# First taps of the tail's depthwise chains made on ScalarE, and a new pace for the work beside the samplings

## The chip, the cores and the metric

The kernel runs on one core of one Trainium2 chip. The metric is device time in microseconds (us), the median of several executions. Engines are named as the profile names them: PE (TensorE's matmuls; PEld its weight loads), DVE (VectorE), ACT (ScalarE), POOL (GpSimd), SP (the queue that issues plain DMAs).

## The reference

Four layers run one after the other on a batch of 4 images of 256 channels and 64 x 64 pixels, all in float32. Each is applied to a group-normalised input and added to its residual:

```python
x = x + L0(_gn(x))   # 1x1 conv; deformable 3x3 sampling in 4 groups (36 points a pixel, bilinear); feed-forward with squeeze-excite
x = x + L1(_gn(x))   # linear attention: qkv 1x1 conv, a 5x5 depthwise conv of qkv, two sums over pixels, projection
x = x + L2(_gn(x))   # 3x3 conv with binarised weights
x = x + L3(_gn(x))   # softmax attention of 4096 pixels to 1024 pooled ones
```

The change bears on three places: the 5x5 depthwise convolution of layer 1 (`agg`), whose 25 taps are summed per channel; the work that runs beside the sampling of layer 0; and the loads of the feed-forward's weights.

## The kernel before, in words

After a head, `run` (from L1348 on) works image by image. `sample(n)` gathers the deformable sampling of image n in 288 rounds: `gathered` issues four indirect DMAs from GpSimd into one of 7 `g` buffers (L607), and PE reduces them with 16 small matmuls (L614). Results are copied by ACT (L619), turned by PE (L624), spread into `dT` by ACT (L634), and, after every 18 rounds, a block is projected (`project`, L647), added to the image (`add`, L653 and L654) and scaled, with a sum for the squeeze-excite mean kept in `ssum` (`finish`, L658).

Beside the rounds of one image, other works of earlier images advance. `beside(steps, number, *works)` takes works as (generator, total cost, lo, hi): after step i of `number`, the share i/number is compared with what each work has spent of its total between lo and hi, and a work that lags is advanced. Costs are numbers written by hand in the generators' `yield`s. Within `ordered()` the instructions of PE, DVE, ACT and POOL run in exactly the order in which the generators write them; the order of SP's DMAs is left to the framework.

- Beside `sample(0)`: the convolution of images 1 to 3 and their offsets.
- Beside `sample(1)`: the binarised weights, then `feedforward(0)` (share 0 to 0.22) and `layer1(0)` (0.22 to 1).
- Beside `sample(2)` and `sample(3)`: `feedforward` and `layer1` of the image before, and `second` of the one before that (layers 2 and 3, from 0.22 to 1).

The feed-forward begins with four loads of weights (L704 to L710: f1 and f2 of 1 MB each, sd, su), takes the mean of `ssum` (L712), goes through two small matmuls (L716, L723), scales f1 on ACT (L727) and then runs its big matmuls (L752, L762). Its buffers lie on the right side of SBUF, where those of `layer1` lay before it.

The tail begins after `sample(3)`. `self.alone` is set, and 900 empty steps carry `feedforward(3)` (share 0 to 0.27), `layer1(3)` (0.27 to 1, cost `LAST`), `layer2(2)` (0.27 to 0.53) and most of `layer3(2)` (from 0.53). Then come `layer2_fours(3)` and `layer3(3)`.

In `layer1`, `chains()` hands out 24 depthwise chains (a padded tile of 16 rows of q, k or v). In the tail two of three go to DVE (`aggregate`, so 16): `depthwise` writes tap 0 with TENSOR_SCALAR (L181) and taps 1 to 24 with SCALAR_TENSOR_TENSOR (L179), which add to `acc` in PSUM, the last one writing to SBUF. The third goes to ACT and POOL (`products`): ACT makes each tap's product (L197), POOL adds it (L201). `step` is called after each of DVE's taps and lets other pieces in: one piece of `later` (transposes, sums, the output's parts), one step of `made` (the qkv rows, every 8 taps) and one step of `aside` (the products, every second tap).

Of the kernel before, what the change touches and what calls it, by code (L numbers as in the profile page):

```python
# [9 lines left out]
F32 = mybir.dt.float32  # L10
I32 = mybir.dt.int32
AF = mybir.ActivationFunctionType
ALU = mybir.AluOpType
# [4 lines left out]
P = 128  # L18
N, C, H, W = 4, 256, 64, 64
# [19 lines left out]

CONVOLVE, OFFSETS, BINARY = NB * 9 + 26, 60, 92  # L40
FEED = NB * 40 + 8
LINEAR, LAST = 956, 582
STEPS, BEGUN = 900, 0.22
CONV2, POOLED = 191, 376.5
CONV, SECOND = 150, 568
EPS_BN = 1e-5
# [26 lines left out]
class Net:  # L73
# [93 lines left out]
        at, n = ROWS[name]  # L167
        return self.rows[:, at:at + n]

    def depthwise(self, acc, src, w, k, rows, cols, r0, bias=None, step=lambda cost: cost, out=None):  # L170


        nc = self.nc
        for t in range(k * k):
            s = src[:, r0 + t // k:r0 + t // k + rows, t % k:t % k + cols]
            wt = w[:, t:t + 1]
            if t:
                to = acc if out is None or t < k * k - 1 else out
                nc.vector.scalar_tensor_tensor(to, s, wt, acc, ALU.mult, ALU.add)  # L179
            elif bias is not None:  # L180
                nc.vector.tensor_scalar(acc, s, wt, bias, ALU.mult, ALU.add)  # L181
            else:
                nc.vector.tensor_scalar(acc, s, wt, None, ALU.mult)
            if self.alone or t % 3 == 2 or t == k * k - 1:
                yield step(1.3 if self.alone else 3.9)

    def products(self, pool, acc, src, w, k, rows, cols, r0, bias, step):

        nc = self.nc
        made = []  # L190
        for t in range(k * k + 3):
            if t < k * k:
                s = src[:, r0 + t // k:r0 + t // k + rows, t % k:t % k + cols]
                m = pool.tile([P, rows, cols], F32, name="m", tag="product", bufs=3) if t else acc
                made.append(m)
                if t:
                    nc.scalar.activation(m, s, AF.Copy, scale=w[:, t:t + 1])  # L197
                else:
                    nc.scalar.activation(m, s, AF.Identity, bias=bias, scale=w[:, t:t + 1])
            if 2 <= t <= k * k:  # L200
                nc.gpsimd.tensor_tensor(acc, acc, made[t - 1], ALU.add)  # L201
            yield step(0.5)


    def setup(self):
# [4 lines left out]
        nc.sync.dma_start(self.cn, a["con"])  # L210
        self.rows = cp.tile([P, NROWS], F32, name="rows")
        nc.sync.dma_start(self.rows, a["rows"])
        self.ow = cp.tile([P, G, C], F32, name="ow")
        nc.sync.dma_start(self.ow, a["outproj_wT"])
        self.ident = cp.tile([P, P], F32, name="ident")
        make_identity(nc, self.ident)
        self.ones = cp.tile([P, P], F32, name="ones")
# [481 lines left out]
    def feedforward(self, n, ssum, st):  # L699
        nc, tc, a = self.nc, self.tc, self.a  # L700
        with tc.tile_pool(name=f"fa{n}", bufs=1, side="right") as sp, \
# [6 lines left out]
            nc.sync.dma_start(sd, a["se_down_wT"])  # L708
            su = sp.tile([64, C], F32, name="su")
            nc.sync.dma_start(su, a["se_up_wT"])  # L710
            mean = sp.tile([P, KT], F32, name="mean")
            nc.vector.tensor_reduce(mean, ssum, AX.X, ALU.add)  # L712
            nc.vector.tensor_scalar(mean, mean, 1.0 / HW, None, ALU.mult)
# [56 lines left out]
    def layer1(self, n, st, st2):  # L770
# [3 lines left out]
        with tc.tile_pool(name=f"la{n}", bufs=1, side="right") as sp, \  # L774
# [10 lines left out]
            ld = sp.tile([P, 4, 2, 32], F32, name="ld")  # L785
            nc.vector.memset(ld, 0.0)

            later, count, aside, every = [], 0, None, 2
            alone = self.alone
            room = lambda bufs, more=1: bufs + more * alone  # L790

            def step(cost, chains=False):


                nonlocal count
                count += chains
                if later and (not alone or count % every or not chains):
                    todo = later.pop(0)
                    todo()
                    cost += 0 if alone else getattr(todo, "cost", 0)  # L800
                if chains:
                    if count % 8 == 6 if alone else count in LEADS:
                        next(made, None)
                    if count % 2 and aside:
                        next(aside, None)
                return cost


# [46 lines left out]
                            if not alone:  # L855
                                yield

            def aggregate(pd, i, name, done, relu=True, **more):

                acc = self.ps1.tile([P, 16, W], F32, name="agg", tag="agg")  # L860
                out = bp.tile([P, 16, W], F32, name=name, tag="ag", bufs=3)
                yield from self.depthwise(acc, pd, self.w5[:, i], 5, 16, W, 0, bias=self.b5[:, i:i + 1],
                                          step=lambda cost: step(cost, True), out=out)
                end(out, done, relu, **more)

            def products(pd, i, name, done, relu=True, **more):

# [4 lines left out]
            def end(out, done, relu, **more):  # L872
                if relu:
                    later.append(lambda: nc.scalar.activation(out, out, AF.Relu, **more))
                done(out)
# [142 lines left out]
            def chain():  # L1018

                while not (args := next(them)):  # L1020
                    yield step(3)
                return args

            while number < 6 * NCH:
                count = 0 if not alone and number % 2 == 0 else count
                *args, more = yield from chain()
                if alone:

                    *slow, smore = yield from chain()
                    aside = products(*slow, **smore)  # L1030
                    yield from aggregate(*args, **more)
                    *args, more = yield from chain()
                    yield from aggregate(*args, **more)
                    for _ in aside:
                        pass
                    number += 3
                else:
                    yield from aggregate(*args, **more)
                    number += 1
            while later:  # L1040
                yield step(1.2 if alone else 1)

# [305 lines left out]
    def run(self):  # L1348
# [2 lines left out]
        ssum = [tile(f"ssum{n}", [P, KT, NBLK]) for n in range(N)]  # L1351
        st = {i: [tile(f"st{i}{n}", [P, KT, NB, 6]) for n in range(2)] for i in (1, 2, 3)}

        feed = lambda n: self.feedforward(n, ssum[n], st[1][n % 2])
        linear = lambda n: self.layer1(n, st[1][n % 2], st[2][n % 2])

        conv = lambda n, side="left": self.layer2(n, st[2][n % 2], st[3][n % 2], side)
# [2 lines left out]
        def second(n):  # L1360
            yield from conv(n)
            yield from pooled(n)

        def beside(steps, number, *works):


            spent, open_ = [0] * len(works), set(range(len(works)))

            def advance(share):
                for j in sorted(open_):  # L1370
                    work, total, lo, hi = works[j]
                    while j in open_ and lo <= share and spent[j] < total * (share - lo) / (hi - lo) or share >= hi:
                        cost = next(work, None)
                        if cost is None:
                            open_.discard(j)
                        if not cost:
                            break
                        spent[j] += cost

            for i, _ in enumerate(steps, 1):  # L1380
                advance(i / number)
            while any(works[j][3] <= 1 for j in open_):
                advance(1)

        rounds = NBLK * BR
        E = mybir.EngineType
        ordered = lambda: self.tc.manual_schedule(engines={E.PE, E.DVE, E.Activation, E.Pool})
        behind = lambda n: [(feed(n), FEED, 0, BEGUN), (linear(n), LINEAR, BEGUN, 1)]
        with self.tc.tile_pool(name="gather", bufs=2, side="left") as self.gp, \
                self.tc.tile_pool(name="samp", bufs=2, side="left") as self.sp:  # L1390
            with self.tc.tile_pool(name="pw", bufs=1, side="right") as wp, \
                    self.tc.tile_pool(name="pa", bufs=1, side="right") as sp, \
                    self.tc.tile_pool(name="pb", bufs=2, side="right") as bp:
                w = self.weights(wp)

                pads, used = [], []  # L1400
                convolved = (y for i in range(1, N) for y in self.convolve(i, w, sp, bp, pads, used))
                shifted = lambda first, last: (self.shifts(first, last, w["mw"], bp, pads, used), (last - first) * OFFSETS)
                beside(range(64), 64, (self.convolve(0, w, sp, bp, pads, used), CONVOLVE, 0, 1), (*shifted(0, 1), 0.3, 1))
                with ordered():
                    beside(self.sample(0, ssum[0]), rounds, (convolved, (N - 1) * CONVOLVE, 0, 0.96), (*shifted(1, N * NCH), 0, 1))
            with ordered():
                beside(self.sample(1, ssum[1]), rounds, (self.binarise(), BINARY, 0, 0.2), *behind(0))
                for n in range(2, N):
                    beside(self.sample(n, ssum[n]), rounds, *behind(n - 1), (second(n - 2), SECOND, BEGUN, 1))
        self.idle, self.alone, self.spare = cycle(["acc", "dp"]), True, True  # L1410
        rest = pooled(N - 2)
        with ordered():
            beside(range(STEPS), STEPS, (feed(N - 1), FEED, 0, 0.27), (linear(N - 1), LAST, 0.27, 1), (conv(N - 2), CONV2, 0.27, 0.53), (rest, POOLED, 0.53, 1.02))
        self.spare = False
        self.idle = cycle(["acc", "dp", "vk"])
        fours = self.layer2_fours(N - 1, st[2][1], st[3][1])
# [99 lines left out]
```

## Time and profile before

| | us |
|---|---|
| median of 3 runs | 7438.36 (7436.6 to 7441.62) |
| profiled execution, device time | 7427.54 |
| its span, first to last instruction | 7425.7 |
| first and last gather of `sample(0)` | 138.5, 1596.4 |
| of `sample(1)` | 1598.0, 3050.3 |
| of `sample(2)` | 3051.6, 4503.0 |
| of `sample(3)` | 4504.2, 5975.5 |
| tail's first big matmul (L752) | 6031.5 |
| first and last of the tail's taps on agg and on its outputs (L179, L181) | 6273.3, 7007.7 |
| first L1211 of `layer2_fours` after the tail's layer 1 | 7086.7 |

The median lies 10.8 us above the profiled execution, which is the one that all traces show. A row of the profile gives a line of the code, the engine, the operation, what it writes and reads, how often, the busy time in us, the mean of one in ns, and then how long the engine sat idle before such instructions and what ended that.

### The profile page before, as it was taken

The numbers are of one execution on the slowest core, as the hardware profiler recorded it, in microseconds if no ns is written. First come the engines' busy times: TensorE is split into PE (matmuls) and PEld (weight loads), VectorE is DVE, ScalarE is ACT, GpSimd is POOL, SyncE is SP. The second block draws the span as 40 slices with busy tenths as digits, with TensorE's granted clock in tenths as the row PEclk, the third lists the DMA queues.
The fourth block names the chain that finished last, engine by engine and source line by source line (L and its number), as shares of the span: only waits on it lengthen the run. The fifth ranks groups of instructions, "written<-read, shape, count | busy, mean of one in ns | idle before, by whom it ended". The sixth has DMA issues, their size and how long they took to land. (4 is left out here: it accounts for less than half of the span.)

```text
span 7425.7 us, 98944 instructions
## 1 busy us (share of the span) xinstructions
PE 5885.9 (79%) x35584; PEld 3436.3 (46%) x35584; DVE 4870.1 (66%) x6099; ACT 3564.6 (48%) x10807; POOL 4928.8 (66%) x4850
## 2 busy tenths in 40 slices
PE   5676766569777777898877788988777889977889
PEld 2333333334433333345655444456554444844477
DVE  6455552644488777326989883269998833999863
ACT  2444444445554444455556554554565532655425
POOL 1777777777777777777777776777777710865410
PEclk7776776779877767898988889989889899988899
DMA  6564654666544445555554445555544431210141
GB/s 187 148 191 144 176 173 137 174 183 190 178 127 125 125 125 147 168 156 167 159 155 139 141 147 187 153 167 159 156 142 145 146 115 65 81 54 34 49 124 49
DMA packets 743149, 1037.48 MB, mean 140 GB/s; under 512 B 352000, under 2 KB 457856, under 8 KB 741248
## 3 DMA queue, kind: packets, MB, share of 16 engines
q0 software_dynamic: 221184, 604.27, 27.8%
q1 hardware_dynamic: 521472, 426.87, 19.0%
q8 instruction: 280, 4.59, 0.3%
q14 instruction: 213, 1.74, 0.1%
HBM read 857.44 MB, written 173.33 MB: 139 GB/s over the span
## 5 line engine op out<-in xcount | busy, mean ns | idle before, releaser
L607 POOL DMA_INDIRECT g<-tab,sl x4608 | 4403.3, 956 | 1571.9 <-issue 1285.6
L179 DVE SCALAR_TENSOR_TENSOR agg<-pad,vec,agg 128x1024 f32<-128x1024 f32 x2280 | 2934.3, 1287 | 64.3
L599 ACT ACTIVATE wm<-sl,con 128x48 f32<-128x48 f32 x6144 | 1496.1, 363 | 24.9 <-DMA sl<-sd 11.8
L614 PE MATMUL dp<-g,wm 128*32 128x128 f32 x9216 | 664.2, 317 | 312.2 <-DMA g<-tab,sl 308.7
L614 PE MATMUL acc<-g,wm 128*32 128x128 f32 x9216 | 664.2, 318 | 298.5 <-DMA g<-tab,sl 285.5
L614 PEld LDWEIGHTS dp<-g,wm 128*32 128x32 f32 x9216 | 324.4, 119 | 664.4 <-DMA g<-tab,sl 493.4
L614 PEld LDWEIGHTS acc<-g,wm 128*32 128x32 f32 x9216 | 325.3, 120 | 661.4 <-DMA g<-tab,sl 452.5
L1102 PE MATMUL ps<-xd,w 128*128 128x256 f32 x2304 | 547.1, 386 | 47.9 <-ACT kt L891 38.6
L1102 PEld LDWEIGHTS ps<-xd,w 128*128 128x128 f32 x2304 | 430.5, 193 | 131.7 <-ACT kt L891 40.3
L752 PE MATMUL ps<-x2f,f 128*128 128x512 f32 x1024 | 479.0, 613 | 4.7 <-ACT f L727 4.0
L762 PE MATMUL ps<-hm,f 128*128 128x512 f32 x1024 | 467.7, 604 | 0.0
L837 PE MATMUL ps<-xr,qw 128*128 128x512 f32 x768 | 442.8, 706 | 31.2 <-DMA xr<-x 20.9
L737 DVE SCALAR_TENSOR_TENSOR hm<-ps,vec,lk 128x512 f32<-128x512 f32 x256 | 191.5, 751 | 372.8 <-ACT lk L754 369.2
L619 ACT COPY at<-dp 128x256 f32<-128x256 f32 x288 | 107.3, 373 | 679.9 <-PE dp L614 668.6
L619 ACT COPY at<-acc 128x256 f32<-128x256 f32 x288 | 107.2, 372 | 594.0 <-PE acc L614 584.0
L754 ACT ACTIVATE lk<-ps,low 128x512 f32<-128x512 f32 x256 | 175.7, 688 | 363.1 <-PE ps L752 359.2
L1333 PE MATMUL ps<-gt,pT 128*128 128x129 f32 x2048 | 303.3, 307 | 34.4 <-ACT pT L1329 32.2
L1333 PEld LDWEIGHTS ps<-gt,pT 128*128 128x128 f32 x2048 | 286.7, 219 | 87.5 <-ACT pT L1329 48.7
L647 PE MATMUL po<-dT,ow 128*128 128x288 f32 x1024 | 299.3, 440 | 25.5 <-ACT dT L642 11.6
L1315 PE MATMUL s<-ph,th 128*128 128x512 f32 x512 | 280.7, 659 | 44.9 <-DVE ot L955 13.8
L201 POOL TENSOR_TENSOR ak<-ak,m 128x1024 f32<-128x1024 f32 x96 | 229.0, 2385 | 119.3 <-ACT m L197 115.7
L201 POOL TENSOR_TENSOR av<-av,m 128x1024 f32<-128x1024 f32 x96 | 227.8, 2373 | 113.2 <-ACT m L197 109.2
(286 smaller groups left out, 8337.6 us busy)
## 6 DMA issues: line engine op xcount, KB each, us to landing
g<-tab,sl POOLq DMA_INDIRECT x4608
x<-x SPq DMA_DIRECT2D x112, 512.0 KB
xr<-x SPq DMA_DIRECT2D x96, 512.0 KB
tab<-xo SPq DMA_DIRECT2D x192, 128.0 KB
x<-in_x SPq DMA_DIRECT2D x32, 512.0 KB
y<-yc SPq DMA_DIRECT2D x32, 512.0 KB
yb<-y SPq DMA_DIRECT2D x64, 256.0 KB
x<-yb SPq DMA_DIRECT2D x64, 256.0 KB
```

The lines of the kernel that those rows point to most:

```text
L179: nc.vector.scalar_tensor_tensor(to, s, wt, acc, ALU.mult, ALU.add)
L201: nc.gpsimd.tensor_tensor(acc, acc, made[t - 1], ALU.add)
L599: nc.scalar.activation(wm[:, :, :, o], blocks[b][:, r:r + WR, G:], AF.Copy, scale=self.con("own")[:, o:o + 1])
L607: nc.gpsimd.indirect_dma_start(out=g[:, i, :], out_offset=None, in_=table, in_offset=bass.IndirectOffsetOnAxis(ap=sl.bitcast(I32)[:, r, i: ...
L614: nc.tensor.matmul(acc[32 * i:32 * i + 32, :], wm[:, r4, 4 * i + 2 * x:4 * i + 2 * x + 2, :], g[:, i, x * P:(x + 1) * P], start=x == 0, st ...
L647: nc.tensor.matmul(po[m][:, 0:BR * OB], self.ow[:, k, m * P:(m + 1) * P], dT[b][:, k].rearrange("p r o -> p (r o)"), start=k == 0, stop=k ...
L752: nc.tensor.matmul(ps, f1[:, k, m * P:(m + 1) * P], x2[:, k], start=k == 0, stop=k == KT - 1)
L762: nc.tensor.matmul(ps, f2[:, k, m * P:(m + 1) * P], hm[:, k], start=k == 0, stop=k == 4 * KT - 1)
L837: nc.tensor.matmul(ps, qw[:, k, m * P:(m + 1) * P], x[:, k], start=k == 0, stop=k == KT - 1)
L1102: nc.tensor.matmul(ps[:, e], w[:, k, t, 2 * half + e, m * P:(m + 1) * P], v[:, 2 * half + e, k, t:t + 8], start=i % 6 == 0, stop=i % 6 == 5)
L1315: nc.tensor.matmul(s[i], tv[:, 4 * b + j], ph[:, i * 512:(i + 1) * 512], start=True, stop=True)
L1333: nc.tensor.matmul(ps[:, 0:P + 1], pT[:, m], gt[:, m], start=m == 0, stop=m == 7)
```

## The change

Seven edits, all of them in one diff:

- In the tail ACT makes the first tap of each chain of DVE (with the bias) into a new SBUF tile `lead` (`begun`); DVE starts at tap 1, whose SCALAR_TENSOR_TENSOR adds to `lead` instead of `acc`. To have it in time, the next chain is fetched during the present one, from its tap 8 on (`fetched`, `FETCH`), and its ACT instruction is written after the next odd tap.
- `ow` moves from the pool that lives to the end to a pool that closes before the tail, and is loaded right after `setup`.
- `aside` advances at 3 of 5 taps instead of every second.
- The tail's constants follow: `LAST` 582 to 558, the convolution's end 0.53 to 0.54.
- In `beside`, with `ahead=True` (samplings 1 to 3): from share 0.86 (round 248) on, the works' share grows at 7/6 of the rounds' pace, reaches 1 at 0.98 (round 282), and nothing is left for the last six rounds.
- `feedforward` has a `yield 1` after its four weight loads.
- `behind(n)` takes the feed-forward of the next image as a fourth work with lo 1 and hi 2: its first step, the four loads, is taken when the works' share has passed 1, and the generator is continued beside the next sampling or in the tail.

```diff
-LINEAR, LAST = 956, 582
-STEPS, BEGUN = 900, 0.22
+LINEAR, LAST = 956, 558
+STEPS, BEGUN, HASTE, END = 900, 0.22, 0.86, 0.98
+LEAD, FETCH = 1, 8
+TAPS = 25 - LEAD
...
-        for t in range(k * k):
+        for t in range(begun, k * k):
...
-                nc.vector.scalar_tensor_tensor(to, s, wt, acc, ALU.mult, ALU.add)
+                nc.vector.scalar_tensor_tensor(to, s, wt, acc if t > begun else lead, ALU.mult, ALU.add)
...
             nc.sync.dma_start(su, a["se_up_wT"])
+            yield 1
...
-                    if count % 2 and aside:
+                    at = count % TAPS
+                    if aside and (3 * at) % 5 < 3:
                         next(aside, None)
+                    if wanted and at >= FETCH:
+                        fetched()
+                    if ahead and at % 2:
+                        next(ahead, None)
...
+            def begun(pd, i, *_):
+
+                made = []
+
+                def taps():
+                    made.append(bp.tile([P, 16, W], F32, name="lead", bufs=1))
+                    yield from self.products(bp, made[0], pd, self.w5[:, i], 5, 16, W, 0, self.b5[:, i:i + 1], lambda cost: cost, LEAD)
+
+                return made, taps()
...
+            if alone:
+                wanted = True
+                for i in range(4 * NCH):
+                    (*args, more), mine = yield from first()
+                    ahead = None
+                    if not i % 2:
+                        *slow, smore = yield from chain()
+                        aside = products(*slow, **smore)
+                    wanted = i + 1 < 4 * NCH
+                    yield from aggregate(*args, lead=mine, **more)
+                    if i % 2:
+                        for _ in aside:
+                            pass
...
-                advance(i / number)
+                share = i / number
+                if ahead and share > HASTE:
+                    share = HASTE + (share - HASTE) * (1 - HASTE) / (END - HASTE)
+                advance(share)
...
-        behind = lambda n: [(feed(n), FEED, 0, BEGUN), (linear(n), LINEAR, BEGUN, 1)]
+        behind = lambda n: [(feeds[n], FEED, 0, BEGUN), (linear(n), LINEAR, BEGUN, 1), (feeds[n + 1], 1, 1, 2)]
...
+            self.ow = self.sp.tile([P, G, C], F32, name="ow", bufs=1)
+            self.nc.sync.dma_start(self.ow, self.a["outproj_wT"])
...
-                beside(self.sample(1, ssum[1]), rounds, (self.binarise(), BINARY, 0, 0.2), *behind(0))
+                beside(self.sample(1, ssum[1]), rounds, (self.binarise(), BINARY, 0, 0.2), *behind(0), ahead=True)
                 for n in range(2, N):
-                    beside(self.sample(n, ssum[n]), rounds, *behind(n - 1), (second(n - 2), SECOND, BEGUN, 1))
+                    beside(self.sample(n, ssum[n]), rounds, *behind(n - 1), (second(n - 2), SECOND, BEGUN, 1), ahead=True)
```

## The prediction

> **What bounds the kernel now.** I read the page first, then busy time by stretch, then the GpSimd queue and the timeline at the two places where it breaks off, then the forms of the tail's instructions.
>
> ```profile
> span 7425.7 us, 98944 instructions
> POOL 1777777777777777777777776777777710865410
> L607 POOL DMA_INDIRECT g<-tab,sl x4608 | 4403.3, 956 | 1571.9 <-issue 1285.6
> L179 DVE SCALAR_TENSOR_TENSOR agg<-pad,vec,agg 128x1024 f32<-128x1024 f32 x2280 | 2934.3, 1287 | 64.3
> ```
>
> GpSimd has the same share from slice 2 to slice 32 but for one 6 (slice 25): the four samplings are a train of 4608 gathers, each 0.95 us and 0.30 us to the next, so a round of four takes 5.0 us. Work beside them costs nothing as long as the train doesn't stop. Behind it comes a tail without gathers, in which VectorE's taps (L179) carry the chain.
>
> ```profile
> core 0: us, PE busy (x) PEld busy (x) DVE busy (x) ACT busy (x) POOL busy (x), PEclk, DMA share, GB/s
> ...
> 4302.00:4502.00 200.00, 163.94 (x1135) 91.80 (x1124) 163.72 (x182) 110.06 (x356) 151.39 (x160) 0.89 0.50 148
> ...
> 5775.00:5945.00 170.00, 141.03 (x961) 78.69 (x960) 142.63 (x160) 90.63 (x299) 128.70 (x136) 0.90 0.48 143
> ...
> 6262.00:6531.00 269.00, 254.71 (x1196) 204.58 (x1196) 229.70 (x300) 157.14 (x223) 202.38 (x101) 0.96 0.29 84
> 6531.00:7058.00 527.00, 401.68 (x1540) 247.50 (x1539) 467.19 (x535) 295.37 (x422) 293.42 (x123) 0.85 0.12 43
> ```
>
> Columns: stretch and length, busy us by engine, granted clock. The second and third rows are the stretches that the new pace squeezes: PE and DVE busy 82 to 84%, neither full. The last two are the tail's layer 1: DVE 85% and 89%, in the first of them PE 95%.
>
> Where the train stops (GpSimd, start and duration, idle before it), at the start of the last sampling:
>
> ```profile
> 4539.27 0.95 POOL L607 DMA_INDIRECT g<-tab,sl  x1 [0.30 <-issue]
> 4553.78 0.94 POOL L607 DMA_INDIRECT g<-tab,sl  x1 [13.57 <-PE acc L614]
> ...
> 4564.49 0.94 POOL L607 DMA_INDIRECT g<-tab,sl  x1 [6.01 <-DMA xyf<-x]
> ```
>
> With smaller gaps of 1.63, 0.85 and 1.22 us that is 23.3 us, or 21.8 over the usual 0.30 each. The sampling's starts span 1471.3 us, the one before it 1451.4. The reason is a lag. From a round's fourth gather to the last L614 matmul on it I count 3 us through most of the second sampling, 12 to 32 us in the later half of the third and fourth, 29.8 us at the fourth's end (5976.46 to 6006.22). There are 7 g buffers of 5 us each, and the longest lag of the third sampling, which hardly stopped, is 34.9: that is the room. The next feed-forward adds some 20 us to a lag of 31: PE waits for its weights.
>
> The end of the last sampling:
>
> ```profile
> 6006.28 0.37 ACT L619 COPY at<-dp 128x256 f32<-128x256 f32 x1 [1.19 <-PE dp L614]
> ...
> 6011.41 0.51 SPq L971 DMA_DIRECT2D x<-xq  x1
> ...
> 6018.56 0.36 SPq L704 DMA_DIRECT2D f<-in_fc_wT  x1
> ...
> 6019.89 0.19 DVE L712 TENSOR_REDUCE mean<-ssum 128x2 f32<-128x32 f32 x1 [0.76 <-ACT yb L658]
> ...
> 6027.79 0.56 PE L716 MATMUL ps<-mean,sd 128*64 128x1 f32 x4 [9.18 <-DMA su<-in_se_up_wT]
> ...
> 6031.50 2.92 PE L752 MATMUL ps<-x2f,f 128*128 128x512 f32 x3 [1.75 <-ACT f L727]
> ```
>
> The last gather ends at 5976.46, the tail's first big matmul starts at 6031.50: 55.0 us, of which 29.8 are lag, 13.7 drain beside leftover work, 7.5 the wait of L716 for weights, and 3.7 the way from L716 to L752.
>
> **The change, part by part.** *Weights ahead.* The four weight loads of a feed-forward are issued at about round 283 of the sampling before it. They can't go before layer 1 has given its memory back: now L704 goes 7.15 us after layer 1's last store (6011.41), and L716 starts 9.2 us after that. SP carries them; its loads of `sl` for a sampling's first block went out some 90 us ahead of it, so they pass in front. `ow` keeps its place among the loads: nothing. Were the weights not ready, the old 7.5 us would be back.
>
> *Pace 7/6 to round 282, then six free rounds.* Nothing is added or removed; 40 rounds' work falls into 34, or 170 us. PE spends some 1.6 us a round on the sampling itself (L614's two groups, 1328 us over 1152 rounds, and the turning and projecting). As the lag neither grows nor shrinks for long at the present pace, I take PE's line of work and waits as full: 5.0 - 1.6 = 3.4 us a round for works. At 7/6 that is 4.0, a round 5.6, and 34 rounds gather 19.4 us of lag. On the 20 us at round 248 this passes the room of 34.9 by 4.5: GpSimd stops for about 5 us in the third and in the fourth sampling, **+10**. In the second sampling, lag 3, nothing. Bounds: nothing, if the idle sixth of PE and DVE takes the denser work; 22 us a sampling, if PE manages only 0.95 of today's pace.
>
> Here a rule can be weighed. The Trainium skill (TensorE: Matmul & The Clock Gate, What's actually happening) says that activity releases the throttle and that the clock is either half or full. The row grants 0.90 on average with PE at 83%, and 1.00 in stretches where PE is full, which fits. By the row's clock the work's 102 us become 119, with 39 of sampling 158 of 170 us; at full clock it would be 142. The rule argues for less lag. I keep the row, since what PE waits for is DVE and ACT, which it doesn't speed.
>
> At the end of a sampling the lag is then 34.9 + 6 x 1.6 - 30 = 14.5 us. Start of the fourth: 14.5 plus a block of 13 to 20 us stays within the room: the stop of **-21.8** goes. What is late next is nothing on GpSimd. End of the fourth: from the last matmul, turn 1.9 (stage 0's last), spread to finish 6.7, mean 0.4, L716 to L752 3.7, together 12.7; with lag 14.5, L752 starts 27.2 us after the last gather. The weights come no later: layer 1's store some 5 us after it, plus 7.15, 9.2 and 3.7, is 25. 55.0 - 27.2: **-27.8**.
>
> *First taps.* Sixteen TENSOR_SCALAR on agg go from DVE, one ACTIVATE each comes to ACT, and the first SCALAR_TENSOR_TENSOR reads that result from SBUF.
>
> ```profile
> L181 DVE TENSOR_SCALAR agg<-pad,vec,b 128x1024 f32<-128x1024 f32 x16 | 21.5, 1344 | 9.8 <-ACT pad L486 9.4
> ```
>
> Two lines by source, with their minimum, median and maximum in ns:
>
> ```profile
> L1280 DVE TENSOR_TENSOR xq<-m x8: 424/426/2459, 6543.9 to 6608.0; 128x256 f32<-128x256 f32 x8
> ...
> L201 POOL TENSOR_TENSOR av<-av,m x96: 2341/2363/2688, 6300.9 to 6905.8; 128x1024 f32<-128x1024 f32 x96
> ```
>
> Removed: 16 x 1.344 = 21.5. Added on ACT: 16 x 1.16 (L197's median) = 18.6, beside an ACT that is busy 57%; issued some 15 taps, 19 us, before they are wanted, so hidden, but for the very first (1.5 us). Without cover, 18.6. Behind a waiting first tap would stand DVE's whole queue: PE's score maxima and convolution results. But the new first tap has both inputs in SBUF while GpSimd adds. L1280 is such an instruction: 0.42 us alone, 2.46 when one of L201's additions runs. The skill (SBUF — State Buffer, SBUF: two separate sides) has the rule: GpSimd and a VectorE instruction with two SBUF inputs take one port pair in turn, each for a whole instruction. Without the rule the gain is 21.5. With it at worst 16 x 2.36 = 37.8 is lost, a loss of 16. The 32 instructions of this kind in the tail (L968, L1277, L1280) took 0.47 us too long on average; GpSimd is busy 56 to 75%, half an addition is 1.2. I take 0.6: 9.6 lost, 11.9 left, and as part of the chains run where PE is 95% busy, **-10**. The side chain's changed beat (3 steps in 5 taps) and the shifted due times move no work: nothing, hidden by DVE's taps.
>
> Sum: +10 - 21.8 - 27.8 - 10 = -49.6. The profiled execution (7427.5, its span 7425.7) would become 7378; it lies 10.8 under the median of the runs, 7438.4, from which I predict 7438.4 - 49.6 = **7389**.
>
> **The rivals.** *The engines keep up* (0.28): PE and DVE have a sixth idle, the clock rises, the six rounds empty the queues. Then no stops, lag 3.2, L752 15.9 us after the last gather (-39.1), taps -14: -75, 7363. For it: DVE held 95% from 5000 to 5100 without a stop. Against: the lag of 20 us that never drains. *The works are the bound* (0.17): at 0.95 of the pace the squeezed stretch loses 37 us, less 15 of room, 22 in each of two samplings: +44 - 21.8 - 27.8 - 10 = -16, 7423; the gain at the boundary was only moved forward. For it: the lag climbs from 17 to 30 over the last 40 rounds. *The pace breaks the train* (0.10), the slower case: steps of works set closer than their latencies hold PE in its written order, and GpSimd behind it. The place is rounds 248 to 282 of the last two samplings, the price 34 us per us that a round exceeds 5.0, less the 15 of room; with 59.6 gained elsewhere it decides from 30 us a sampling, 6.3 us a round. At 7.0 it is +106 - 59.6 = +46, 7485. Against: the present 5.0 contains idle time. *Moved taps gain nothing* within the forecast's case: 7399, or 7415 with every tap blocked.
>
> **The numbers.** The forecast has 0.42; 0.03 stay for what I don't see. A change within 0.2%, 15 us, is about what a measurement can't tell from none. Faster by more (under 7423.5): the forecast, the first rival and half of the second, 0.78; same 0.12; slower 0.10. The range goes from the first rival with all the taps' worth, 7354, past the second, to 7436, leaving out the slower case.
>
> **What would show it.** No gap over 5 us in the gathers near 4550; stops before L607 by PE, some 5 us in all, in the last 40 rounds of samplings three and four (none: first rival; over 20: second; over 30: third). From last gather to the first L752 about 27 us instead of 55, with L716 not waiting for a DMA. In the tail no L181 on agg, but 16 first taps of 1.3 to 3.7 us, and layer 1 done 10 us sooner after L752's start. I am wrong if the train's stops move instead of vanishing, or if the tail lengthens.

## The result, and the profile after

The changed kernel takes 7457.6 us, median of 9 runs (7452.7 to 7466.6); the kernel before takes 7436.6 beside it, also 9 runs. The ratio is 1.003, 95% interval [1.002, 1.004]: slower by 0.3%, where the prediction had it faster by 0.7%. In the two profiled executions the tail's first big matmul starts 15.1 us earlier than before (6031.5 to 6016.4), and the tail from there to the end takes 46 us longer (1394.2 to 1440.1). So the prediction is right about the boundary between the last sampling and the tail, which gives 26 us, and wrong about the tail.

The page of the kernel after, the same rows as were shown of before (line numbers have moved: L181 now is the SCALAR_TENSOR_TENSOR of the taps, L183 the old tap 0, L753 the feed-forward's first matmuls, L717 its first small matmul):

```profile
span 7456.5 us, 98965 instructions
POOL 1777777777777777777777777777777702865310
L607 POOL DMA_INDIRECT g<-tab,sl x4608 | 4411.4, 957 | 1574.7 <-issue 1283.4
L181 DVE SCALAR_TENSOR_TENSOR agg<-pad,vec,agg 128x1024 f32<-128x1024 f32 x2264 | 2912.9, 1287 | 63.7
```

The one 6 in GpSimd's row, where the last sampling began, has gone. Busy time by stretch, the squeezed stretches first, then the tail's layer 1 in its two parts (us; PE, PEld, DVE, ACT, POOL, then granted clock):

```profile
4302.00:4502.00 200.00, 168.41 (x1125) 92.67 (x1126) 171.12 (x194) 106.62 (x336) 148.66 (x158) 0.91 0.50 147
...
5775.00:5945.00 170.00, 147.46 (x988) 82.24 (x987) 153.61 (x172) 94.44 (x295) 126.44 (x133) 0.92 0.49 146
...
6247.00:6516.00 269.00, 256.60 (x1195) 204.22 (x1194) 226.17 (x283) 170.27 (x235) 214.21 (x104) 0.97 0.27 76
6516.00:7086.00 570.00, 422.15 (x1536) 252.52 (x1536) 455.80 (x536) 302.47 (x425) 286.45 (x120) 0.84 0.13 43
```

The squeezed stretches are denser, as meant (DVE 84% to 90% in the second). The last two rows carry the loss. The first part of layer 1 takes its 269 us as before. The second takes 570 instead of 527, with less work on DVE (455.8 us instead of 467.2): its share falls from 89% to 80%. An engine that did less waited more. PE has as many matmuls (1536 and 1540), and is busy with them for 422 us instead of 402.

GpSimd's larger stops in the samplings (start, duration, idle before it); two at the start of the last sampling, then those of its last 80 us:

```profile
4526.64 1.26 POOL L607 DMA_INDIRECT g<-tab,sl  x1 [1.93 <-PE dp L614]
...
4563.82 0.94 POOL L607 DMA_INDIRECT g<-tab,sl  x1 [2.17 <-PE ps L753]
```

```profile
5919.11 0.94 POOL L607 DMA_INDIRECT g<-tab,sl  x1 [0.49 <-PE acc L614]
5940.48 0.95 POOL L607 DMA_INDIRECT g<-tab,sl  x1 [1.49 <-PE acc L614]
5957.07 0.94 POOL L607 DMA_INDIRECT g<-tab,sl  x1 [1.86 <-PE acc L614]
5977.73 0.94 POOL L607 DMA_INDIRECT g<-tab,sl  x1 [5.96 <-PE dp L614]
```

The stop of 13.57 + 6.01 us near 4550 is now 1.93 + 2.17; in its place stand stops at the end. Against the usual 1.25 us a gather, the first 48 rounds of the last sampling lose 4.0 us (before 21.8), its rounds from 272 on 10.7 (before 0.9), those of the third sampling 9.7 (before 0.3). Over their whole length the third and fourth samplings lose 51 us, before 45: the stops have moved, and GpSimd's train has become no shorter.

The end of the last sampling, the timeline of the kernel after:

```profile
6012.46 0.55 SPq L661 DMA_DIRECT2D x<-yb  x1
6012.47 0.19 DVE L713 TENSOR_REDUCE mean<-ssum 128x2 f32<-128x32 f32 x1 [0.76 <-ACT yb L658]
...
6012.96 0.36 PE L717 MATMUL ps<-mean,sd 128*64 128x1 f32 x4 [1.77 <-issue]
...
6016.43 1.22 PE L753 MATMUL ps<-x2f,f 128*128 128x512 f32 x1 [2.16 <-ACT f L728]
```

The last gather starts at 5986.5, so L753 comes 29.9 us after it (before 56.0, both counted from the gather's start), and the small matmul no longer waits for a DMA.

The tail's first taps and the others, by form, and what DVE waited for in the tail's layer 1, after and then before (us in all, times, longest):

```profile
L181 DVE SCALAR_TENSOR_TENSOR agg<-pad,vec,agg 128x1024 f32<-128x1024 f32 x352 | 452.1, 1284 | 8.0
...
L181 DVE SCALAR_TENSOR_TENSOR agg<-pad,vec,lead 128x1024 f32<-128x1024 f32 x16 | 25.3, 1584 | 13.0 <-ACT lead L201 12.3
```

```profile
DVE rden L1372 <- PE ps L1369: 42.7, 18, 4.7
DVE mx L1352 <- PE s L1351: 22.2, 25, 4.1
...
DVE agg L181 <- ACT lead L201: 12.3, 1, 12.3
```

```profile
DVE rden L1336 <- PE ps L1333: 18.3, 9, 4.7
...
DVE agg L181 <- ACT pad L486: 9.4, 1, 9.4
DVE mx L1316 <- PE s L1315: 8.5, 18, 3.8
```

The first taps do what was meant: 1.58 us on average, where another tap takes 1.28, 16 times, and only the very first waits, 12.3 us, where before the same chain waited 9.4 for its pad. The first chain ends 305.4 us after the first big matmul (before 304.7), so this is not the loss. (Before, its first tap starts at 6283.2 us; 6273.3 in the table of times is the start of its wait.) Even the sixth of the 16 chains ends at 508.5 (before 510.4). The last one ends at 1004.0 (976.2), and layer 2 of image 3 begins at 1100.5 (1055.2): 28 us are lost in the chains that run beside layer 3 of image 2, and 17 behind the last chain.

Most of DVE's added waiting is in two other rows: `mx` waits for `s` and `rden` for `ps`. Both belong to layer 3 of image 2. They held DVE for 26.8 us before and for 64.9 after, 38 of the 60 us by which DVE's idle time grew in the two windows of these rows (825 us before, 870 after).

Behind the last chain no tap is left to stand in the queue. The two stretches from its end to layer 2 of image 3, before and after:

```profile
7007.70:7086.70 79.00, 59.85 (x235) 32.96 (x233) 38.17 (x76) 29.41 (x44) 0.00 (x0) 0.94 0.50 155
```

```profile
7020.40:7116.90 96.50, 75.18 (x248) 40.97 (x246) 38.90 (x77) 30.01 (x45) 0.00 (x0) 0.85 0.41 127
```

DVE and ACT have nearly the same work there. PE has 13 matmuls more, is busy 15 us longer, and its granted clock is 0.85 instead of 0.94.

### The profile page after: what moved, and what is told of

The parts are those of the page before. It is cut to its first block, busy times and chain, and to the rows that moved or that the text cites. A ratio compares the mean times of both kernels' runs of the same rounds, so it can differ in the third digit from the quotient of the medians.

```text
span 7456.5 us, 98965 instructions
## 1 busy us (share of the span) xinstructions
PE 5899.8 (79%) x35584; PEld 3432.7 (46%) x35584; DVE 4852.2 (65%) x6083; ACT 3586.3 (48%) x10823; POOL 4941.8 (66%) x4850
## 5 line engine op out<-in xcount | busy, mean ns | idle before, releaser
L181 DVE SCALAR_TENSOR_TENSOR agg<-pad,vec,agg 128x1024 f32<-128x1024 f32 x2264 | 2912.9, 1287 | 63.7
L844 PE MATMUL ps<-xr,qw 128*128 128x512 f32 x768 | 461.7, 732 | 44.7 <-DMA xr<-x 25.1
L753 PE MATMUL ps<-x2f,f 128*128 128x512 f32 x1024 | 477.9, 612 | 4.8 <-ACT f L728 4.4
L1369 PE MATMUL ps<-gt,pT 128*128 128x129 f32 x2048 | 299.9, 304 | 51.2 <-ACT pT L1365 47.3
L1351 PE MATMUL s<-ph,th 128*128 128x512 f32 x512 | 282.7, 662 | 45.1 <-DVE ot L972 13.8
```

What stands on the lines that cost most here:

```text
L181: nc.vector.scalar_tensor_tensor(to, s, wt, acc if t > begun else lead, ALU.mult, ALU.add)
L753: nc.tensor.matmul(ps, f1[:, k, m * P:(m + 1) * P], x2[:, k], start=k == 0, stop=k == KT - 1)
L844: nc.tensor.matmul(ps, qw[:, k, m * P:(m + 1) * P], x[:, k], start=k == 0, stop=k == KT - 1)
L1351: nc.tensor.matmul(s[i], tv[:, 4 * b + j], ph[:, i * 512:(i + 1) * 512], start=True, stop=True)
L1369: nc.tensor.matmul(ps[:, 0:P + 1], pT[:, m], gt[:, m], start=m == 0, stop=m == 7)
```

## The experiments

What layer 3 is: for each of 32 pixel tiles, one step after another, PE makes scores `s`, DVE their maximum `mx`, ACT the exponentials `pe`, PE turns them (`pt`), ACT copies (`pT`), PE sums (`ps`), DVE takes the reciprocal `rden`, ACT scales (`m`). Eight hand-overs a tile; in the tail they are written between DVE's taps, and every engine takes its instructions in the order in which they are written. From the first `mx` to the last `m`, the 32 tiles take 455 us before, 14 us each, and 491 after; they also start 12 us later, counted from the first big matmul.

**My theory in the end:** in that stretch no engine's busy time is the bound but the way of layer 3 through PE, DVE and ACT in the written order. Any edit that shifts taps against layer 3's steps, or takes taps away, makes DVE arrive at `mx` or `rden` early and wait, with its taps behind it. **Rivals:** the moved tap itself costs (port, `lead`); layer 3's later start costs (0.54); DVE bounds the tail after all, and the loss comes from elsewhere. "Tail" below means the time from the first big matmul of the last feed-forward to the end, in the profile; ratios are to the kernel before on the same chip, with the 95% interval. Each tail length is that of one profiled execution. Of long lines of code only the part that changes is shown.

### Cutting the change in two

`e1_pace_only` is the kernel before with the three edits of the samplings (pace, `yield 1`, weights ahead):

```diff
+                if ahead and share > HASTE:
+                    share = HASTE + (share - HASTE) * (1 - HASTE) / (END - HASTE)
...
+            yield 1
...
+(feeds[n + 1], 1, 1, 2)]
```

> The kernel before with only the new pace (7/6 from round 248, six free rounds) and the weights ahead; the tail as it was. Theory A (the tail's chain edits cost 46 us, the pace gained some 15 to 20): 15 to 20 us under the kernel before, about 7418. Rival B (the pace or the weights ahead leave something behind that lengthens the tail): as slow as the changed kernel, 20 over the kernel before.

Measured: 7414.2 us, 0.9963 [0.9949, 0.9978]; tail 1392.8.

`e2_tail_only` is the kernel after without pace and without weights ahead:

```diff
-*behind(0), ahead=True)
+*behind(0))
...
-(linear(n), LINEAR, BEGUN, 1), (feeds[n + 1], 1, 1, 2)]
+(linear(n), LINEAR, BEGUN, 1)]
```

> The changed kernel with the old pace and the weights loaded as before; only the tail's edits and the place of ow remain. Theory A: some 35 to 45 us over the kernel before, and the time from the tail's first L753-type matmul to the end 1440 instead of 1394. Rival B: within 10 us of the kernel before.

Measured: 7487.6 us, 1.0061 [1.0044, 1.0078]; tail 1442.0. So the samplings' part gains 28.5 us and the tail's part loses 44.9. Their sum is +16.4; the whole change was measured at +21.0.

### Which edit of the tail

`e3_old_beat`, the kernel after with the products at every second tap again:

```diff
-                    if aside and (3 * at) % 5 < 3:
+                    if aside and count % 2:
```

> The changed kernel with the side chain advanced at every second tap again. Theory A1 (the denser beat of 3 in 5 taps crowds ScalarE and makes layer 3's steps late): 20 to 40 us faster than the changed kernel. Theory A2 (layer 3 runs beside 16 taps fewer, and its dependent steps stand closer together): within 10 us of the changed kernel.

Measured: 7449.7, 1.0009 [1.0000, 1.0018]; tail 1432.2, so 7.9 us of the loss are the beat's, though with the old beat the 16 first taps take more of DVE (34.7 us instead of 25.3).

`e4_loop_no_lead`, the kernel after with tap 0 on DVE again, while the new loop (next chain fetched ahead), the beat and 0.54 stay:

```diff
-LEAD, FETCH = 1, 8
+LEAD, FETCH = 0, 8
...
-LINEAR, LAST = 956, 558
+LINEAR, LAST = 956, 582
...
-                    lead, ahead = begun(*then)
+                    lead, ahead = None, None
...
```

> The changed kernel with tap 0 back on VectorE (no instruction on ScalarE, 25 taps, LAST 582), with the chains still fetched ahead and the new beat. If the moved tap and its shorter count cost the time (A2, or the lock of the port): about 7420, like the pace alone. If fetching ahead or the beat cost it: stays within 15 us of the changed kernel, 7440 to 7470.

Measured: 7443.8, 1.0000 [0.9992, 1.0009]; tail 1422.3. No tap is moved here, and the tail still is 29.5 us longer than that of the pace alone. That rules out the moved tap as the whole cause.

Then single edits on `e1_pace_only`. `f1_pace_054`:

```diff
-(conv(N - 2), CONV2, 0.27, 0.53), (rest, POOLED, 0.53, 1.02)
+(conv(N - 2), CONV2, 0.27, 0.54), (rest, POOLED, 0.54, 1.02)
```

> The pace alone with one tail constant changed: layer 2's end and layer 3's start at 0.54 instead of 0.53. Theory D (the tail is held by layer 3's dependent steps, and any denser packing of them beside layer 1's taps costs): 8 to 15 us over the pace alone, about 7425. If the order in which the chains are fetched is the cause: no change, 7414 to 7418.

`f2_pace_beat`:

```diff
-                    if count % 2 and aside:
+                    if aside and (3 * (count % 25)) % 5 < 3:
```

> The pace alone with the side chain at 3 of 5 taps. From the step between the changed kernel and its old beat (13 us in the runs): about 10 us over the pace alone, 7424, if the beat acts by itself; nothing if it acts only together with the moved tap's ScalarE work.

`f3_pace_ahead`: e4 with the old beat and 0.53, so that only the new loop is left.

> The pace alone with the new loop: chains fetched from tap 8 of the one before, old beat, 0.53, tap 0 on VectorE. Theory F (fetching ahead pulls layer 1's row steps and pads to other places and is what costs): 15 to 25 us over the pace alone. Theory D: within 5 us of it.

`g1_lead_old_beat_053`: the kernel after with the old beat and 0.53.

> The changed kernel with the old beat and 0.53: the moved tap, its fetching ahead and LAST 558 are all that is left in the tail. Theory D: it falls between the pace alone and the old-beat run, about 7435, as layer 3 still has 16 taps fewer beside it. If the moved tap alone were worth its 12 us and only beat and start cost: 7402.

These four ran on another chip, on which the kernel before takes 8512 us, all of it more in the samplings; so their ratios compare only with each other. Measured: f1 0.9961 [0.9949, 0.9973], tail 1406.1; f2 0.9969 [0.9957, 0.9981], 1407.8; f3 0.9966 [0.9958, 0.9975], 1406.6; g1 0.9980 [0.9972, 0.9989], 1417.3. Three edits that add no instruction each seemed to make the tail 13 to 15 us longer. For f3 the theory of that time had allowed 5: it saw only a denser layer 3 as a cost, and that was too narrow. That they were so alike could as well have been the chip. So the pace alone and f1 were run again on one chip:

> The control for all tail lengths that were read on different chips: the kernel before with the pace and the weights ahead, once more. If a tail (first feed-forward matmul to end) is the same on every chip, as the theory has it, it is 1393 +- 3 us here too, whatever the samplings take. The rival, that a chip with slower samplings also has a slower tail by some 13 us, expects 1404 to 1408 if this chip's before is above 8000 us, and 1393 if it is near 7440. Ratio to before on this chip: 0.996.

> The same kernel with one number changed, layer 3's start at a share of 0.54 instead of 0.53. Theory, layer 3 is bound to the written order: tail 13 us longer than that of the pace alone on the same chip, 1406 +- 3, ratio to before 0.998. Rival, the 13 us measured earlier belong to the chip: the tail is within 3 us of that of the pace alone on the same chip (1393 on a chip whose before is near 7440, both 1406 on the other kind), ratio 0.996.

Measured: q1 7403.1, 0.9963 [0.9949, 0.9977], tail 1391.8; q2 7423.8, 0.9985 [0.9975, 0.9995], tail 1405.2. The tail is the same on both kinds of chip within 1 us, and one number moved from 0.53 to 0.54 costs 13.4 us. (f2 and f3 were not repeated.) DVE's waits in the tail's layer 1, q1 and then q2:

```profile
DVE rden L1337 <- PE ps L1334: 18.6, 9, 4.7
...
DVE mx L1317 <- PE s L1316: 8.5, 18, 3.8
```

```profile
DVE rden L1337 <- PE ps L1334: 25.2, 14, 4.7
DVE mx L1317 <- PE s L1316: 21.4, 21, 5.2
```

The same two rows as in the change: 27.1 us become 46.6.

Is it that layer 3 starts late? `n1_pace_052` starts it earlier:

```diff
-(conv(N - 2), CONV2, 0.27, 0.53), (rest, POOLED, 0.53, 1.02)
+(conv(N - 2), CONV2, 0.27, 0.52), (rest, POOLED, 0.52, 1.02)
```

> The pace alone with layer 2's end and layer 3's start at 0.52 instead of 0.53 (0.54 made the tail 13.3 us longer). If a late start of layer 3 is what costs: 5 to 13 us less, tail about 1383. If 0.53 only happens to be a good order and every other one is worse: 5 to 15 us more.

Measured, on a chip like that of f1 (before 8583.8): 0.9976 [0.9966, 0.9986], tail 1414.3, which is 21.5 us longer than at 0.53. Earlier is worse than later, so lateness alone is not the cause. The tail by parts (us) shows that the two neighbours of 0.53 lose in different places:

| | to the end of DVE's sixth chain | to the end of its last | to layer 2 of image 3 | to the end |
|---|---|---|---|---|
| 0.53 (q1) | 508.7 | 465.1 | 79.1 | 338.8 |
| 0.54 (q2) | 498.9 | 487.2 | 80.3 | 338.8 |
| 0.52 (n1) | 521.1 | 472.3 | 81.8 | 339.0 |
| the whole change (after) | 508.5 | 495.5 | 96.5 | 339.6 |

The first part holds layer 2 of image 2, and PE is nearly full there. Its second half, from 240 us after the first big matmul on, of q1 and q2:

```profile
6246.10:6514.80 268.70, 253.87 (x1194) 203.57 (x1193) 236.95 (x301) 159.50 (x229) 204.09 (x101) 0.96 0.27 78
```

```profile
6248.80:6507.70 258.90, 246.03 (x1174) 197.77 (x1173) 234.55 (x285) 156.78 (x221) 205.00 (x101) 0.98 0.26 75
```

With 0.54 the first six chains end 9.8 us sooner, beside 20 matmuls less, and the part beside layer 3 takes 22.1 longer. With 0.52 they end 12.4 later, more than half of that kernel's loss, and layer 3's part takes 7.2 longer. A due time thus does move work, between a stretch where PE is full and one where layer 3 runs.

### The tap, with and without layer 3

`h1_tap_left_out` is e1 with tap 0 left out of the 16 chains of DVE in the tail (its bias goes into tap 1; the step after it stays, so all else keeps its place). It leaves out part of the convolution:

```diff
+            if self.alone and not t:
+                pass
+            elif self.alone and t == 1:
+                nc.vector.tensor_scalar(acc, s, wt, bias, ALU.mult, ALU.add)
-            if t:
+            elif t:
```

> The pace alone, with tap 0 of VectorE's sixteen chains in the tail left out of the sum (its step in the written order stays, without an instruction; tap 1 takes the bias). Everything else stands as in the pace alone, whose tail from the first feed-forward matmul to the end was 1392.8 us. If VectorE's taps bind the tail (as predicted): 16 to 21 us less, about 1373. If layer 3's dependent steps bind it (theory D): under 6 us less.

Measured: 7400.5, 0.9950 [0.9934, 0.9967], tail 1387.3. DVE has 16 instructions less, 16.9 us of busy time between 240 us after the first big matmul and the end of layer 1, and the tail is 5.5 us shorter. That is what was expected if layer 3 binds (under 6).

`h2_lead_25_steps` is f3 with the tap on ACT, but with 25 steps a chain and `LAST` 582 kept (an empty step where tap 0 was):

```diff
-        for t in range(begun, k * k):
+        for t in range(k * k):
...
-            if t:
+            if t < begun:
+                pass
+            elif t:
```

> The fetching-ahead run with tap 0 on ScalarE, but with 25 steps a chain, LAST 582, the old beat and 0.53, so that the order of all else is that run's (tail 1406.6 us). If the shorter count is what costs (layer 3 packed against 16 taps fewer): the moved tap shows its worth, 8 to 12 us less, about 1396. If ScalarE's sixteen instructions or the shared port cost it: 1407 to 1417, like the run with the lead, old beat and 0.53 (1417.3).

Measured: 7419.3, 0.9975 [0.9966, 0.9985], tail 1403.4: 3.2 us shorter than f3, where 8 to 12 were expected. g1 differs from h2 in the count alone (24 steps, 558) and takes 13.9 longer. Its last chain ends at the same time (985.6 and 985.2 us after the first big matmul); the way from there to layer 2 of image 3, with the same ten score maxima in it, takes 92.5 us instead of 78.7. PE is busy for 68.8 us of it (239 matmuls, granted clock 0.87), in h2 for 58.8 (236 matmuls, 0.95): 10 of the 14 us are PE's.

Now the same without layer 3. `m1_no_layer3`, `m2_no_layer3_tap_out` and `m3_after_no_layer3` are e1, h1 and the changed kernel, each without layer 3 of image 2:

```diff
-        rest = pooled(N - 2)
+        rest = iter(())
```

> The pace alone with layer 3 of the third image left out of the tail, here and in the last stretch (its part of the output isn't written). It is the base for the two runs beside it. Layer 1's last chain ends earlier than the pace alone's 973.8 us after the first feed-forward matmul: by some 80 us if its VectorE work (about 90 us of 742) is all that it took, by more if its dependent steps also made VectorE wait.

> The run without layer 3 and with tap 0 of the tail's sixteen VectorE chains left out, its step kept. Theory D (VectorE binds layer 1 only as long as layer 3's chain of dependent steps isn't beside it): the last chain ends 17 to 21 us sooner than in the run without layer 3, against 5.8 us with layer 3. If VectorE isn't the bound there either: under 8 us.

> The changed kernel, with layer 3 of the third image left out in the same way. Theory D: the tail's edits cost only because layer 3 runs beside them, so without it the last chain ends 8 to 15 us sooner than in the run without layer 3 (predicted worth of the moved taps: 12). If fetching ahead, the beat or ScalarE's load cost by themselves: 10 us or more later.

| | with layer 3 of image 2: tail | without it: tail |
|---|---|---|
| pace alone (e1, m1) | 1392.8 | 1299.4 |
| the same, tap 0 left out (h1, m2) | 1387.3 | 1289.0 |
| the whole change (after, m3) | 1440.1 | 1287.9 |

Ratios of the three without layer 3, which leave out work: 0.9828 [0.9810, 0.9846] for m1, 0.9820 [0.9798, 0.9843] for m2, 0.9825 [0.9805, 0.9844] for m3; they can't be told apart, since their spread is wider than 10 us on this chip, so the tails of the profiles decide. Without layer 3 the change makes the tail 11.5 us shorter. With it, 47.3 longer. Leaving the tap out gives 10.4 without layer 3, 5.5 with it; 17 to 21 had been expected without it if DVE were the bound there, and under 8 if not. Leaving layer 3 out of the pace alone ends the last chain 89.3 us sooner, while DVE has 64 us less to do up to there: the other 25 were waits. Busy time of equal stretches of 330 us, from 540 us after the first big matmul on, of q1, of the kernel after, and of m1:

```profile
6546.10:6876.10 330.00, 245.25 (x964) 160.50 (x963) 304.94 (x338) 201.50 (x288) 209.29 (x88) 0.83 0.11 37
```

```profile
6556.40:6886.40 330.00, 234.55 (x930) 149.61 (x928) 284.14 (x325) 201.25 (x283) 200.48 (x84) 0.86 0.12 39
```

```profile
7694.80:8024.80 330.00, 143.72 (x368) 59.35 (x368) 321.47 (x287) 161.31 (x180) 252.82 (x107) 0.68 0.08 24
```

The third column of busy times is DVE: 92%, 86%, and 97% without layer 3. Only the last of these is nearly full. Of the 16.5 us of work that m2 has less than m1, 10.4 come back as time; of the 16.9 in h1, 5.5. In both, the first tap starts 4 to 5 us later than with tap 0 in place, so part of the loss has nothing to do with layer 3. Two stretches of layer 1, of e1 and of h1, each from the end of DVE's tenth chain to the end of its last (680 to 974 us after the first big matmul in e1, 674 to 968 in h1):

```profile
6696.80:6990.80 294.00, 224.53 (x827) 135.72 (x828) 270.40 (x298) 161.61 (x223) 172.06 (x72) 0.84 0.11 36
```

```profile
6690.70:6984.70 294.00, 224.11 (x827) 135.71 (x828) 264.41 (x291) 161.76 (x222) 172.01 (x73) 0.84 0.11 36
```

The same 827 matmuls take the same 294 us, though DVE has 6 us less to do.

### The pace

`k1_pace_early` starts the pace at share 0.60 instead of 0.86 (1.05 times instead of 7/6); `k2_pace_no_weights` is e1 without the loads ahead:

```diff
-STEPS, BEGUN, HASTE, END = 900, 0.22, 0.86, 0.98
+STEPS, BEGUN, HASTE, END = 900, 0.22, 0.60, 0.98
```

> The pace alone with the faster pace from round 173 (share 0.60) instead of 248, so 1.05 times instead of 7/6. If the room of seven buffers is what the 7/6 pace overruns: the stops of 9.7 and 10.7 us in rounds 272 to 288 of the last two samplings shrink to under 4 each, 10 to 15 us under the pace alone. If the works are the bound, the lag has grown by then all the same: within 5 us.

```diff
-(linear(n), LINEAR, BEGUN, 1), (feeds[n + 1], 1, 1, 2)]
+(linear(n), LINEAR, BEGUN, 1)]
```

> The pace alone without the weights ahead. From last gather to the first feed-forward matmul 37 us instead of 30 (the 7.5 us that the small matmul waited before), and at the start of the fourth sampling a stop of under 10 us, since the lag there is 16 instead of 31: 7 to 15 us over the pace alone.

Measured: k1 7406.1, 0.9958 [0.9941, 0.9974], tail 1392.5; k2 7407.2, 0.9961 [0.9947, 0.9976], tail 1393.5. Neither the 10 to 15 us that k1 might have gained nor the 7 to 15 that k2 should have lost are there. In k1 the stops leave the last rounds (3.3 us from 272 on, in both samplings) and appear in rounds 144 to 248 (14.9 and 14.5 us; e1 6.7 and 6.3). In all, the third and fourth samplings lose 24.4 and 25.0 us, in e1 23.4 and 27.8, in the kernel before 12.7 and 32.6: stops are moved, not removed. What the pace gains is the 26 us behind the last gather. In k2 the last gather to the first big matmul takes 30.0 us, as in e1: there L704 goes at 5993.4 us, 3.1 after layer 1's last store and 15.0 ahead of L717. With the pace, layer 1 ends early enough for the loads to be in time at their old place. k1, k2 and e1 all beat both kernels; they can't be told from each other.

## Why the prediction was wrong, step by step

- *Stops of the pace, +10.* Right in mechanism, half in size: 9.7 and 10.7 us in the rounds from 272 on, against 5 each; less the 0.3 and 0.9 that were there before, +19.
- *The stop at the start of the fourth sampling, -21.8.* Right: 4.0 of it are left, -17.8. The smaller lag does it, for in k2, without the loads ahead, the stop is gone as well. But with the +19 the train as a whole gained nothing, where I had it gain 11.8.
- *Drain to the first big matmul, -27.8.* Right: -26.1. "Were the weights not ready, the old 7.5 us would be back" is wrong: k2 loads them at the old place, and still in time.
- These three sum to -25. Between the two profiled executions the first big matmul comes only 15.1 us sooner: the other 10 us are small stops elsewhere, 2.2 and 2.8 in the first two samplings and 5 in the last two. Such stops differ between executions (the first sampling took 1462.0 us in e1 and 1456.9 in q1, the same kernel). In the medians the pace alone gave -28.5 and -30.8 (e1, q1).
- *First taps, -10.* The price of a two-input first tap was no constant: 0.30 us more than the other taps on average in the changed kernel, 0.89 with the old beat (e3, g1). I took 0.6 from L1280 and the Trainium skill's rule on the shared port pair (SBUF — State Buffer, SBUF: two separate sides). The rule agrees with the trace: seven of the 16 met a running addition of GpSimd and ended 1.1 us after it. That 0.6 lies between the two is luck. The gain of about 10 is there when layer 3 is not (m3, -11.5 with all the tail's edits). Beside layer 3 the step at unchanged count gains 3.2 (h2 against f3).
- *"The side chain's changed beat (3 steps in 5 taps) and the shifted due times move no work: nothing, hidden by DVE's taps."* **This is the step that failed**, and with it the fetch ahead, which I had costed by its first wait alone. Taken one after another from the pace alone, the edits give: fetch ahead +13.8 (f3), tap on ACT -3.2 (h2), 24 steps and `LAST` 558 +13.9 (g1), 0.54 +14.9 (e3), beat +7.9 (after): +47.3 together. Alone, the beat costs 15.0 and 0.54 13.4. They don't add up in a fixed way, as prices of orders and not of instructions. A shifted due time doesn't leave the work in its place either: with 0.54 the stretch where PE is full loses 20 matmuls and the one with layer 3 grows by 22 us.
- Behind it lies a reading. I took "DVE 85% and 89%" for the bound of the tail's layer 1, so that work moved off DVE was gain and reordering was hidden. But with layer 3 beside it an 89% busy DVE was an engine in a chain of hand-overs whose order fitted. Without layer 3 it is 97% busy, and there the reading comes nearer: 10.4 of 16.5 us taken off DVE come back.
- Of the rivals, none was this one. I had placed the slower case in the pace ("steps of works set closer than their latencies hold PE in its written order"): the mechanism was near, the place was not. Both of my signs of being wrong came: the train's stops moved, and the tail lengthened.

What stays open: the traces show that DVE waits longer at `mx` and `rden`, that layer 3 has to be there, and that moves without work do it. That it is the order on each engine which turns a shift into a wait is argued from that. Leaving layer 3 out also takes 197 us of PE's busy time away (q1 and m1, from the sixth chain's end to layer 2 of image 3), so those runs don't separate its hand-overs from its load on PE. Which step meets which tap was not followed one by one. A rival that no run tests is PE's granted clock: it doesn't explain 0.54, where PE is busy no longer than at 0.53, but in the whole change PE is busy 25 us longer in layer 1 for the same matmuls, at 0.87 instead of 0.89, and 15 of these lie behind the last chain. Whether the lower clock makes the waits there or follows from them is not shown. Layer 3 with its scores one tile ahead, which should make the tail less touchy, was not tried.

## What to carry to other kernels

Where several engines follow one written order and one of the interleaved works is a serial chain over three of them, "moves no work" is no reason for "costs nothing": price a reordering from both sides, by the hand-overs of that chain (here 13 to 21 us for a start shifted by 1% of the steps). Take an engine for the bound only when it is about full and its waits are few: here it was 89% busy, with recurring waits on the same two partners, and of 16.9 us of work taken off it 5.5 came back. When an edit bundles a schedule change with a gain elsewhere, look whether the halves can be had apart: the pace alone gives 0.9963 [0.9949, 0.9978].

## What the hardware showed that I had not expected

The same kernel took 7434 to 7443 us on some chips and 8512 and 8584 on others. The difference is all in the samplings: one gather takes 0.955 us on both kinds (f1 and q2), but GpSimd sits idle before its gathers for 2624 us in f1 and for 1576 in q2, while the tails are 1406.1 and 1405.2. The rows of the gathers, f1 and then q2:

```profile
L607 POOL DMA_INDIRECT g<-tab,sl x4608 | 4399.2, 955 | 2624.2 <-issue 1195.8
```

```profile
L607 POOL DMA_INDIRECT g<-tab,sl x4608 | 4402.2, 955 | 1576.3 <-issue 1284.6
```

What makes the one kind slower there the runs don't tell. A second surprise is how much the price of a two-input first tap depends on the moment. Nine of the changed kernel's 16 took 1.27 to 1.29 us, as any other tap. The other seven started while GpSimd had at least half a microsecond of an addition left, and each ended 1.1 us after that addition did. The longest of them, with the addition that it met:

```profile
6403.14 2.36 POOL L203 TENSOR_TENSOR ak<-ak,m 128x1024 f32<-128x1024 f32 x1 [0.27 <-DVE av L181]
```

```profile
6403.24 3.34 DVE L181 SCALAR_TENSOR_TENSOR agg<-pad,vec,lead 128x1024 f32<-128x1024 f32 x1
```

So the average, 1.58 us here and 2.17 in e3 and g1, is a matter of how the beat places GpSimd's additions against DVE's first taps.
